# A four-layer block of scan, experts and attention on one core: normalised rows on ScalarE, shared experts as a queue behind, one copy per scatter

## The chip, the cores and the metric

The kernel runs on one core of a Trainium2 chip. The metric is the time of one execution on the device in microseconds; of the kernel before, three executions took 1660.49, 1661.27 and 1664.24 us, and their median, 1661.27 us, is the time before.

The core has five engines with queues of their own, which meet through semaphores only. The profile calls them PE (TensorE, matrix products; PEld is its loading of weights), DVE (VectorE), ACT (ScalarE), POOL (GpSimd) and SP (SyncE, which here issues DMAs). An engine works through its queue in order: an instruction that waits holds up all that stand behind it on that engine.

## The reference

The input x has 8 batches of 512 rows of 256 numbers in float32. Four layers are added to it one after the other, each on the normalised rows:

```python
x = x + _L0_attn_a_ref(_layernorm(x, axis=-1), ...)   # a scan over the 512 rows
x = x + _L0_ffn_ref(_layernorm(x, axis=-1), ...)      # a mixture of experts
x = x + _L0_attn_b_ref(_layernorm(x, axis=-1), ...)   # causal attention, 16 heads of 16
x = x + _L0_ffn_ref(_layernorm(x, axis=-1), ...)      # the same mixture, same weights
```

`_layernorm` is `(x - m) / jnp.sqrt(v + eps)`, without weights. The scan projects to 512 channels, keeps a decaying sum of each, and projects back. The attention clips its scores to -10 to 10, masks and takes a softmax. The mixture is

```python
topk_idx, tw = _route(x, router_w, bias)              # 4 of 16 experts per row, with gains
h = jnp.einsum('td,edf->etf', x, gate_w)
u = jnp.einsum('td,edf->etf', x, up_w)
y = jnp.einsum('etf,efd->etd', jax.nn.silu(h) * u, down_w)
routed = jnp.einsum('etd,te->td', y, combine)
sh = jax.nn.silu(x @ sh_gate_w) * (x @ sh_up_w) @ sh_down_w   # two shared experts, every row
return (routed + sh).reshape(hidden_states.shape)
```

## The kernel before

**Stages.** `stretch(Scan())` runs the scan layer for all 8 batches, and with it everything of the first mixture but the chosen experts: the route of every batch and the shared experts. `routed(0, ...)` then runs the chosen experts on blocks of 128 rows that were sorted by expert in HBM (`xg`). `stretch(Attention())` and `routed(1, ...)` do the same for the third and fourth layer. In `routed` a block's rows are loaded (L982 to L986), turned, multiplied (L1029, L1059) and added to `part` in HBM by an indirect DMA of GpSimd (L1069). At its start it needs the last scatter into `xg` and the table of blocks that `blocks` makes (L906, L915).

**A stretch.** Its loop takes the batches in turn. In iteration b the main work of batch b (`layer.main`) is woven together with the projection of batch b + 1 (Attention), the normalisation and turning of a coming batch (`norm(nxt)`, `turn(nxt)`), the route of batch b - 1 (`Route`: its norm, its scores and the chain of small VectorE steps in `choices`), the scatter of the sorted rows of batch b - 2, and some of the shared experts. The weaving is an order of program: `beside` lets several pieces of work advance evenly by matmul columns, and `timed` puts each step of a piece at a given fraction of the iteration. The Tile framework then fixes each engine's order from that.

**The shared experts.** `shared_experts` (L1142 for gate and up, L1170 for down) costs TensorE the same for each batch: 12 units of 1024 columns, 96 units in a stretch. `quota` says how many units stand beside an iteration: the first number holds for b = 2 to 6, the second for the last iteration, the third for the piece behind the loop, in which the last batch's route is made; what is left goes beside the final piece, with the last scatters and the table of blocks. The results are stored to `part` (L1180). The transposed rows that they read come from the route. In Scan the rows of batches 0 to 5 are kept at the end of `w_all`, in the place of the last two (`OUT`) experts' weights (`kept_rows`, three places in turn); those two experts are loaded once batch 5 is done (`done_with`). In Attention the rows stay in one of the `kb4` buffers (nine of them, shared with much else), and `w_all` from expert 5 on holds the attention's scores and projections (`spot`); these experts are loaded again after the loop (`end`).

**Normalised rows.** `normed` makes mean and variance on VectorE (L469, L470), raises the variance to -0.5 on GpSimd (L489), and forms the rows on VectorE, one instruction for each of four tiles of 128 rows (L494): subtract the mean, multiply by the factor. With `by_vector` the root is made on VectorE as well; the last route of each stretch and the two batches that `prepared` handles during `routed(0)` do so.

**Scatters.** For each route 16 indirect DMAs on GpSimd (L794) put 128 rows each into `xg`, at places that stand in `slots`. So that they do not all start at once, the places are copied to `slots` by ScalarE, in pairs (`PACE = 2`, L791): the copies are pinned in ScalarE's order, and a scatter cannot start before its copy. The last route of Attention is not paced: one VectorE copy (L773) gives all 16 places.

Of the kernel before, what the change touches and what calls it, by code (L numbers as in the profile page):

```python
# [61 lines left out]
PACE = 2  # L62
SENT = 4
# [20 lines left out]
def tile_hybrid_block(  # L84
# [351 lines left out]
    def by_shares(src, tag: str, into, into_rows: bool):  # L436


        rows = src()
        through = dram.tile([T, D], FP, name=f"through_{tag}")  # L440
        nc.sync.dma_start(out=through.rearrange("(t p) d -> p t d", p=P), in_=rows)
        share = rows.rearrange("p t d -> p (t d)") if into_rows else kb4(f"share_{tag}").rearrange("p t d -> p (t d)")
        for a in range(QUAD):
            nc.sync.dma_start(
                out=share[a * SQ : (a + 1) * SQ, :].rearrange("s (g c) -> s g c", g=T // SQ),
                in_=through[:, a * KD * SQ : (a + 1) * KD * SQ].rearrange("(g s) c -> s g c", s=SQ),
            )
        yield 0
        dst = work.tile([P, KD, T], FP, tag="kb4", name=f"xT_{tag}", bufs=KB)
        into(dst)  # L450
        for half in range(2):
            g = slice(half * T // SQ // 2, (half + 1) * T // SQ // 2)
            nc.vector.transpose(
                dst.rearrange("p k (g s) -> p k g s", s=SQ)[:, :, g],
                share.rearrange("p (g i k) -> p k g i", i=SQ, k=KD)[:, :, g],
            )
        yield 0
# [4 lines left out]
    def normed(b: int, tag: str, place, by_vector: bool = False, pinned: bool = False, past=lambda: None):  # L462
# [27 lines left out]
        xn = place()  # L490
        for t in range(NT):
            with tc.issue_after(past().ins) if past() is not None else nullcontext():
                keep(
                    nc.vector.tensor_scalar(  # L494
                        xn[:, t, :], x_sb[:, t, :], mv[:, t, 0:1], rstd[:, t : t + 1], ALU.subtract, ALU.mult
                    )
                )
            yield
# [24 lines left out]
    class Scan:  # L523
        mixture, ahead, copies, turns = 0, 1, by_scalar, (0.75, 0.79)
        quota = (10, 10, 20)
        early = 0
# [89 lines left out]
    class Route:  # L616
# [3 lines left out]
        def __init__(self, i: int, b: int, copies):  # L620
            self.i, self.b, self.tag, self.copies = i, b, f"m{i}_{b}", copies
            self.held = {}
            self.rest = choices(i, b, self.tag, self.held, i == 0 or b < B - 1)
# [11 lines left out]
        def norm(self, by_vector: bool = False):  # L635
# [3 lines left out]
            return normed(self.b, self.tag, self.place, by_vector, past=past)  # L639

        def scores(self, shares: bool = False):
            if shares:
                yield from by_shares(
                    lambda: self.held["rows"][:, :, 0:D], self.tag, lambda xnT: self.held.update(xnT=xnT), False
# [542 lines left out]
    first_expert = E - -(-(ES + QK) * NT * D // WEXP)  # L1187
# [8 lines left out]
    class Attention:  # L1196
        mixture, ahead, copies, turns = 1, 2, by_both, (0.65, 0.85)
        quota = (12, 6, 18)
# [5 lines left out]
        def done_with(self, b: int):  # L1204
            pass

        def end(self):
            for e in range(first_expert, E):
                load_expert(e)
# [207 lines left out]
    def stretch(layer):  # L1417
# [5 lines left out]
        def norm(b: int, first: bool = False):  # L1423
# [4 lines left out]
            return normed(b, f"l{i}_{b}", place, False, first)  # L1428
# [70 lines left out]
        for b in range(1 if begun else 0, B):  # L1499
# [10 lines left out]
            if b > 1:  # L1510
                shared_sum = experts(layer.quota[last])
                fill.append(shared_sum)
                pieces.append(timed(sends.pop(), 0.1, 0.14, 0.18, *spread(0.22, 0.66 if last else 0.86, NT * TK)))
            if fill:
                pieces.append(behind(*fill))
            if b > 0:
# [7 lines left out]
                if last:  # L1524
# [3 lines left out]
                        timed(some(r.rest, 3 + SENT), 0.79, 0.81, 0.83, *spread(0.85, 1.0, SENT)),  # L1528
# [18 lines left out]
            if i == 0 and b == 2:  # L1547
# [7 lines left out]
        chain = 3 + PICKS  # L1555
        issue(
# [3 lines left out]
                timed(sends.pop(), *spread(0.0, 0.5, NT * TK - SENT)),  # L1560
                timed(r.scores(), 0.2, 0.22, *spread(0.28, 0.33, NT)),
                timed(some(r.rest, chain + 8), *spread(0.36, 0.68, chain), *spread(0.7, 1.0, 8)),
# [6 lines left out]
                timed(r.rest, *spread(0.0, 0.5, NT * TK - 8)),  # L1569
# [103 lines left out]
```

## Time and profile before

| | us |
|---|---|
| median of three runs | 1661.27 |
| the profiled execution, on the device | 1663.38 |
| its span from first to last instruction | 1661.7 |
| TensorE busy | 1583.4 (95%) |
| VectorE busy | 1004.3 (60%) |
| ScalarE busy | 766.2 (46%) |
| GpSimd busy | 762.9 (46%) |
| the 256 scatters (L794), GpSimd busy | 258.4 |
| the 120 copies that pace them (L791) | 21.3 |
| matmuls of the shared experts end (Scan, Attention) | 349.9, 1266.0 |

The busy times come from one profiled execution; ends of matmuls are modelled, so a busy TensorE is not TensorE at its peak. PEclk is the share of its full clock that TensorE was granted. In a list of groups the columns are line, engine, operation, what is written from what, count, then busy time in us and mean ns of one, then the engine's idle time before them and who ended it. In a timeline a row is start, duration, engine, line and operation, with the idle time before it and its releaser in brackets. A table by stretches gives for each engine its busy us and its count of instructions.

### The profile page before, as it was taken

What the parts mean: (1) busy time and instruction counts of PE and PEld (TensorE: products, weight loads), DVE (VectorE), ACT (ScalarE), POOL (GpSimd) and SP (SyncE); (2) the same over time, 40 slices, a digit from 0 to 9 for tenths busy, and PEclk for the clock granted to TensorE, in tenths of its full rate; (3) what the DMA queues carried; (4) which work ended last, traced back from release to release, by engine and by line L of the source; (5) the groups of instructions that cost most, each with busy time, mean ns of one, the idle gap of its engine ahead of it and who ended that gap; (6) DMA issues with size and microseconds to landing.
All of it is one profiled execution on the core that took longest, in us unless ns stands there. A gap on an engine that the chain in (4) does not pass through costs nothing. (4 is left out here: it accounts for less than half of the span.)

```text
span 1661.7 us, 33893 instructions
## 1 busy us (share of the span) xinstructions
PE 1583.4 (95%) x10030; PEld 1162.3 (70%) x10030; DVE 1004.3 (60%) x3265; ACT 766.2 (46%) x1486; POOL 762.9 (46%) x639
## 2 busy tenths in 40 slices
PE   8899998999999999999999999999888999999996
PEld 5466655579999999973344444445447999999995
DVE  6777765434466444438988878868643444545553
ACT  3333432235555555556554444444113555555553
POOL 4456646525556555540032332322552555555554
PEclk9999998999999999999999999999899999999998
DMA  5444424447777766641324234232643776787776
GB/s 167 168 147 146 156 92 146 164 83 105 117 122 107 104 99 97 88 72 39 89 90 120 88 109 117 79 110 78 228 156 72 107 123 109 131 140 135 133 136 131
DMA packets 281644, 195.30 MB, mean 118 GB/s; under 512 B 168592, under 2 KB 262064, under 8 KB 281456
## 3 DMA queue, kind: packets, MB, share of 16 engines
q1 hardware_dynamic: 228896, 119.93, 28.2%
q0 software_dynamic: 51984, 72.09, 24.3%
q8 instruction: 85, 1.39, 0.4%
q10 hardware_dynamic: 576, 1.05, 0.2%
q14 instruction: 103, 0.84, 0.2%
HBM read 89.71 MB, written 103.23 MB: 116 GB/s over the span
## 5 line engine op out<-in xcount | busy, mean ns | idle before, releaser
L1069 POOL DMA_INDIRECT part<-rows x272 | 425.9, 1566 | 341.4 <-ACT rows L1068 246.0
L794 POOL DMA_INDIRECT xg<-sorted_m,slots_m x256 | 258.4, 1009 | 274.4 <-ACT slots_m L791 75.6
L1029 PEld LDWEIGHTS ph<-rows,gate 128*128 128x128 f32 x2160 | 277.6, 191 | 33.5 <-ACT rows L1012 22.0
L1029 PE MATMUL ph<-rows,gate 128*128 128x128 f32 x2160 | 291.6, 278 | 1.7 <-ACT rows L1012 1.7
L1029 PE MATMUL ph<-rows,up 128*128 128x128 f32 x2160 | 285.3, 275 | 0.0
L1059 PE MATMUL pyr<-w_all,rows 128*128 x1088 | 279.3, 380 | 0.0
L1029 PEld LDWEIGHTS ph<-rows,up 128*128 128x128 f32 x2160 | 262.9, 192 | 0.0
L1002 DVE COPY up<-w_all 128x512 f32 x270 | 119.5, 443 | 225.1 <-PE ph L1029 201.1
L1002 ACT COPY gate<-w_all 128x512 f32 x270 | 166.5, 617 | 123.7 <-DVE up L1002 59.6
L1039 DVE TENSOR_TENSOR rows<-ph,rows 128x256 f32<-128x256 f32 x272 | 115.3, 424 | 151.3 <-ACT rows L1037 80.9
L1291 ACT ACTIVATE w_all<-ps_a 128x1024 f32<-128x1024 f32 x160 | 155.1, 1021 | 104.3 <-PE ps_a L1281 97.8
L1059 PEld LDWEIGHTS pyr<-w_all,rows 128*128 128x128 f32 x1088 | 186.9, 192 | 14.3
L1068 ACT ACTIVATE rows<-pyr,gain 128x256 f32<-128x256 f32 x272 | 128.7, 473 | 77.7 <-PE pyr L1059 58.1
L1037 ACT ACTIVATE rows<-ph 128x256 f32<-128x256 f32 x272 | 104.3, 383 | 116.7 <-PE ph L1029 99.1
L1170 PE MATMUL pd_m<-sd_sb,act_m 128*128 128x256 f32 x512 | 124.5, 391 | 13.3 <-DVE act_m L1158 7.6
L1170 PEld LDWEIGHTS pd_m<-sd_sb,act_m 128*128 128x128 f32 x512 | 97.9, 195 | 40.5 <-issue 11.4
L1281 PE MATMUL ps_a<-w_all 32*128 32x384 f32 (+3 forms) x1024 | 106.6, 475 | 8.8 <-ACT w_all L1291 8.5
L1301 DVE SCALAR_TENSOR_TENSOR w_all<-w_all,causal 128x512 f32<-128x512 f32 (+1 forms) x160 | 91.5, 572 | 38.3 <-ACT w_all L1291 36.4
L1317 PE MATMUL po_a<-w_all,v_a 128*32 128x512 f32 (+3 forms) x1024 | 92.8, 452 | 0.3 <-issue 0.3
L1281 PEld LDWEIGHTS ps_a<-w_all 32*128 32x128 f32 x1024 | 45.0, 188 | 66.6 <-ACT w_all L1291 34.5
L1016 DVE STREAM_TRANSPOSE rows<-rows 128x256 f32<-128x256 f32 x180 | 78.8, 438 | 5.6 <-issue 2.6
L1142 PE MATMUL pg_m<-xT_m,sg_sb 128*128 128x512 f32 x160 | 78.0, 610 | 0.0
(223 smaller groups left out, 1937.8 us busy)
## 6 DMA issues: line engine op xcount, KB each, us to landing
rows<-xg SPq DMA_DIRECT2D x720, 32.0 KB
rows<-xg SPq DMA_DIRECT2D x92, 134.0 KB
part<-x SPq DMA_DIRECT2D x16, 512.0 KB
part<-ys_m SPq DMA_DIRECT2D x14, 512.0 KB
sum<-part SPq DMA_DIRECT2D x14, 512.0 KB
w_all<-in_L_ffn_gate_w_dram SPq DMA_DIRECT2D x27, 256.0 KB
w_all<-in_L_ffn_up_w_dram SPq DMA_DIRECT2D x27, 256.0 KB
w_all<-in_L_ffn_down_w_dram SPq DMA_DIRECT2D x27, 256.0 KB
```

The lines of the kernel that those rows point to most:

```text
L794: nc.gpsimd.indirect_dma_start(out=xg[i], out_offset=bass.IndirectOffsetOnAxis(ap=slots[:, at : at + 1], axis=0), in_=rows[:, t, :], in_of ...
L1002: copy(here, w_all[:, bass.ds(held[n][0] + half * KD * F, KD * F)])
L1029: nc.tensor.matmul(ph[s][:, f * P : (f + 1) * P], lhsT=both[s][:, k * F + f * P : k * F + (f + 1) * P], rhs=rows[:, ROW + k * P : ROW + (k ...
L1037: nc.scalar.activation(act, ph[0], AF.Silu)
L1039: made = nc.vector.tensor_mul(act, ph[1], act)
L1059: nc.tensor.matmul(py, lhsT=act[:, f * P : (f + 1) * P], rhs=w_all[:, bass.ds(w + 2 * KD * F + f * D, D)], start=(f == 0), stop=(f == KF - 1),
L1068: nc.scalar.mul(y, py, gain[:, TK : TK + 1])
L1069: acc = nc.gpsimd.indirect_dma_start(out=parts[i][n % 2], out_offset=bass.IndirectOffsetOnAxis(ap=rows[:, D + 2 * TK : D + 2 * TK + 1].bit ...
L1170: nc.tensor.matmul(py[:, j, :], lhsT=acts[n][:, f, t * P : (t + 1) * P], rhs=shared[n][3][:, f, :], start=(n == 0 and f == 0), stop=(n == ...
L1281: nc.tensor.matmul(ps[j // 2][:, j % 2, col : col + n], lhsT=k_sb[w][r, o, c * P : (c + 1) * P], rhs=q_sb[r, o, c * P : T], start=True, st ...
L1291: nc.scalar.activation(es[two], ps[two], AF.Exp, scale=ATT_SCALE)
L1317: nc.tensor.matmul(at["po", w][32 * j : 32 * j + 32, c * P : T], lhsT=v_sb[:, c, h * VC : h * VC + 32], rhs=at[w, c, j], start=(c == place ...
```

## The change

1. `normed` takes `by_scalar_too`. In Attention, for the layer's own norms (batches 2 to 7) and for routes 0 to 6, VectorE makes one small offset, minus the mean times the factor, and ScalarE forms the four tiles as Identity of factor times x plus offset.
2. Attention's quota becomes (10, 8, 20). Its transposed rows of routes 0 to 5 go to `kept_rows` at the end of `w_all`; the attention's own places move down by two experts, and the last two experts are loaded again when batch 5 of the shared experts is done.
3. `PACE` is 1, and the last route of Attention is paced too. In Scan the last 4 of a route's 16 scatters move to the first sixth of the next iteration (`over`), the other 12 spread up to 0.97; no scatter of route 6 stands in the last iteration any more (`sent`), and 4 instead of 8 of route 7's stand before the final piece (`begun_last`). Attention keeps its numbers there.

```diff
@@ -59,8 +59,7 @@
 CLIP = 10.0
 KB, COLS = 9, 6
 HALVED = 1597463007.0
-PACE = 2
-SENT = 4
+PACE = 1
 OUT, STAY = 2, 3
 AHEAD = 6
 BY_PE = 3
@@ -433,7 +432,7 @@
             copies[k](dst[:, k, :], flat)
             yield T // 2
 
-    def by_shares(src, tag: str, into, into_rows: bool):
+    def by_shares(src, tag: str, into, into_rows: bool, home=None):
 
 
         rows = src()
@@ -446,7 +445,7 @@
                 in_=through[:, a * KD * SQ : (a + 1) * KD * SQ].rearrange("(g s) c -> s g c", s=SQ),
             )
         yield 0
-        dst = work.tile([P, KD, T], FP, tag="kb4", name=f"xT_{tag}", bufs=KB)
+        dst = home() if home else work.tile([P, KD, T], FP, tag="kb4", name=f"xT_{tag}", bufs=KB)
         into(dst)
         for half in range(2):
             g = slice(half * T // SQ // 2, (half + 1) * T // SQ // 2)
@@ -459,7 +458,9 @@
     by_both = (nc.scalar.copy, nc.vector.tensor_copy)
     by_scalar = (nc.scalar.copy, nc.scalar.copy)
 
-    def normed(b: int, tag: str, place, by_vector: bool = False, pinned: bool = False, past=lambda: None):
+    def normed(
+        b: int, tag: str, place, by_vector=False, pinned=False, past=lambda: None, by_scalar_too=False
+    ):
 
         keep = tc.keep_in_program_order if pinned else lambda made: made
         x_sb = x_tiles[b]
@@ -488,6 +489,15 @@
             keep(nc.vector.tensor_scalar(rstd, mv[:, :, 1], EPS, None, ALU.add))
             powers[tag] = nc.gpsimd.tensor_tensor(rstd, rstd, neg_half, ALU.pow)
         xn = place()
+        if by_scalar_too:
+            off = small.tile([P, NT], FP, tag="minus", name=f"minus_{tag}")
+            nc.vector.scalar_tensor_tensor(off, mv[:, :, 0], -1.0, rstd, ALU.mult, ALU.mult)
+            for t in range(NT):
+                nc.scalar.activation(
+                    xn[:, t, :], x_sb[:, t, :], AF.Identity, scale=rstd[:, t : t + 1], bias=off[:, t : t + 1]
+                )
+                yield
+            return
         for t in range(NT):
             with tc.issue_after(past().ins) if past() is not None else nullcontext():
                 keep(
@@ -523,6 +533,7 @@
     class Scan:
         mixture, ahead, copies, turns = 0, 1, by_scalar, (0.75, 0.79)
         quota = (10, 10, 20)
+        over, sent, begun_last = 4, 0, 4
         early = 0
 
 
@@ -620,7 +631,7 @@
         def __init__(self, i: int, b: int, copies):
             self.i, self.b, self.tag, self.copies = i, b, f"m{i}_{b}", copies
             self.held = {}
-            self.rest = choices(i, b, self.tag, self.held, i == 0 or b < B - 1)
+            self.rest = choices(i, b, self.tag, self.held, True)
 
         def place(self):
             rows = work.tile([P, NT, ROW], FP, tag="rows", name=f"sorted_{self.tag}")
@@ -636,12 +647,18 @@
 
 
             past = (lambda: gained.get(self.b - 1)) if self.i == 0 else lambda: None
-            return normed(self.b, self.tag, self.place, by_vector, past=past)
+            return normed(
+                self.b, self.tag, self.place, by_vector, past=past, by_scalar_too=self.i == 1 and not by_vector
+            )
 
         def scores(self, shares: bool = False):
             if shares:
                 yield from by_shares(
-                    lambda: self.held["rows"][:, :, 0:D], self.tag, lambda xnT: self.held.update(xnT=xnT), False
+                    lambda: self.held["rows"][:, :, 0:D],
+                    self.tag,
+                    lambda xnT: self.held.update(xnT=xnT),
+                    False,
+                    (lambda: kept_rows(self.b)) if self.b < B - 2 else None,
                 )
                 yield from logits(self.i, self.b, self.tag, self.held)
                 return
@@ -1184,7 +1201,7 @@
 
 
 
-    first_expert = E - -(-(ES + QK) * NT * D // WEXP)
+    first_expert = E - OUT - -(-(ES + QK) * NT * D // WEXP)
     spots = {"es": [0, ES, 0], "qk": [ES, QK, 0]}
 
     def spot(kind: str, rows: int):
@@ -1195,17 +1212,17 @@
 
     class Attention:
         mixture, ahead, copies, turns = 1, 2, by_both, (0.65, 0.85)
-        quota = (12, 6, 18)
+        quota = (10, 8, 20)
+        over, sent, begun_last = 0, 4, 8
         early = 2
         norms, scores, choose = (0.0, 0.12, 0.2, 0.28), (0.29, 0.45, 0.55, 0.6), (0.66, 0.95)
         last_rows, last_scores = (0.2, 0.28), (0.35, 0.38)
         bursts, parts = {}, {}
 
-        def done_with(self, b: int):
-            pass
+        done_with = Scan.done_with
 
         def end(self):
-            for e in range(first_expert, E):
+            for e in range(first_expert, E - OUT):
                 load_expert(e)
 
         def load(self, b: int):
@@ -1425,7 +1442,7 @@
                 xn[b] = kb4(f"xn_{i}_{b}")
                 return xn[b]
 
-            return normed(b, f"l{i}_{b}", place, False, first)
+            return normed(b, f"l{i}_{b}", place, False, first, by_scalar_too=i == 1)
 
         def turn(b: int, copies=layer.copies):
             if i == 1 and b >= layer.ahead:
@@ -1510,7 +1527,14 @@
             if b > 1:
                 shared_sum = experts(layer.quota[last])
                 fill.append(shared_sum)
-                pieces.append(timed(sends.pop(), 0.1, 0.14, 0.18, *spread(0.22, 0.66 if last else 0.86, NT * TK)))
+                if len(sends) > 1:
+                    pieces.append(timed(sends.pop(0), *spread(0.0, 0.16, layer.over)))
+                wait = 0.16 if i == 0 and b == 2 else 0.0
+                first = [wait + place for place in (0.1, 0.14, 0.18)]
+                if layer.over:
+                    pieces.append(timed(some(sends[0], 3 + NT * TK - layer.over), *first, *spread(0.22 + wait, 0.97, NT * TK - layer.over)))
+                else:
+                    pieces.append(timed(sends.pop(), *first, *spread(0.22, 0.66 if last else 0.86, NT * TK)))
             if fill:
                 pieces.append(behind(*fill))
             if b > 0:
@@ -1525,7 +1549,7 @@
                     pieces += [
                         timed(r.scores(), *layer.last_scores, *spread(0.5, 0.56, NT)),
                         timed(some(r.rest, PICKS), *spread(0.57, 0.67, PICKS - 1), 0.76),
-                        timed(some(r.rest, 3 + SENT), 0.79, 0.81, 0.83, *spread(0.85, 1.0, SENT)),
+                        timed(some(r.rest, 3 + layer.sent), 0.79, 0.81, 0.83, *spread(0.85, 1.0, layer.sent)),
                     ]
                 else:
                     pieces += [
@@ -1553,20 +1577,24 @@
 
         r = start_route(B - 1)
         chain = 3 + PICKS
+        many = layer.begun_last
+        left = [timed(sends.pop(0), *spread(0.0, 0.14, layer.over))] if layer.over else []
+        within = (0.16, 0.8) if layer.over else (0.0, 0.5)
         issue(
             beside(
                 experts(layer.quota[2]),
                 timed(r.norm(by_vector=True), *spread(0.0, 0.05, 2 * NT)),
-                timed(sends.pop(), *spread(0.0, 0.5, NT * TK - SENT)),
+                *left,
+                timed(sends.pop(), *spread(*within, NT * TK - layer.sent)),
                 timed(r.scores(), 0.2, 0.22, *spread(0.28, 0.33, NT)),
-                timed(some(r.rest, chain + 8), *spread(0.36, 0.68, chain), *spread(0.7, 1.0, 8)),
+                timed(some(r.rest, chain + many), *spread(0.36, 0.68, chain), *spread(0.84 if layer.over else 0.7, 1.0, many)),
             )
         )
         table = []
         issue(
             beside(
                 Piece((B * 12 - (B - 3) * layer.quota[0] - sum(layer.quota[1:])) * each, whole),
-                timed(r.rest, *spread(0.0, 0.5, NT * TK - 8)),
+                timed(r.rest, *spread(0.0, 0.65 if layer.over else 0.5, NT * TK - many)),
                 timed(blocks(i, table), 0.03, 0.14, 0.26, 0.38),
             )
         )
```

## The prediction

> **What bounds the kernel now.** I read the page's slices first, then the table by stretches cut where the line numbers of the timeline change: 0 to 351 us is Scan, 351 to 741 the first run of sorted blocks, 741 to 1267 Attention, then the second run of blocks and the landing of its last sums.
>
> ```profile
> PE   8899998999999999999999999999888999999996
> PEclk9999998999999999999999999999899999999998
> ```
>
> ```profile
> core 0: us, PE busy (x) PEld busy (x) DVE busy (x) ACT busy (x) POOL busy (x), PEclk, DMA share, GB/s
> ...
> 241.00:280.00 39.00, 32.35 (x126) 21.67 (x125) 23.24 (x85) 10.49 (x25) 18.05 (x18) 0.87 0.21 72
> 280.00:351.00 71.00, 68.40 (x248) 40.65 (x246) 27.13 (x105) 17.80 (x40) 29.74 (x33) 1.00 0.50 156
> ...
> 794.00:840.00 46.00, 42.78 (x325) 18.79 (x322) 42.14 (x124) 23.93 (x31) 3.58 (x5) 0.96 0.31 85
> ...
> 900.00:962.00 62.00, 59.61 (x393) 29.04 (x390) 50.89 (x148) 28.34 (x45) 20.09 (x21) 1.00 0.36 107
> ...
> 1148.00:1198.00 50.00, 45.50 (x279) 19.49 (x280) 36.96 (x121) 16.76 (x33) 20.12 (x21) 0.86 0.53 181
> 1198.00:1267.00 69.00, 57.42 (x216) 35.47 (x215) 31.83 (x119) 9.41 (x21) 28.61 (x31) 0.95 0.41 132
> ```
>
> TensorE sets the time nearly everywhere; a middle iteration of Attention (900 to 962) keeps it busy 59.6 of 62 us. Its lost time lies at the ends of the two stretches. Counting idle time plus (1 - granted clock) of the stretch: 241 to 280 loses 6.7 + 5.1 = 11.7 us, 1148 to 1198 loses 4.5 + 7.0 = 11.5, 1198 to 1267 loses 11.6 + 3.5 = 15.1. I then looked at TensorE's timeline there:
>
> ```profile
> 270.38 0.69 PE L743 MATMUL pr_m<-sel_m,tri 128*128 128x64 f32 x2 [6.65 <-DVE sel_m L735]
> ```
>
> ```profile
> 1174.83 1.01 PE L1317 MATMUL po_a<-w_all,v_a 128*32 128x512 f32 x1 [0.34 <-issue]
> 1178.78 2.99 PE L1281 MATMUL ps_a<-w_all 32*128 32x128 f32 x16 [2.93 <-ACT w_all L1291]
> ```
>
> ```profile
> 1248.79 2.27 PE L906 MATMUL pe_b<-chosen_b,cand_e 128*128 128x143 f32 x8 [7.96 <-DVE chosen_b L895]
> ```
>
> Three holes: 6.7, about 3 and 8.0 us. GpSimd's timeline shows what they share: each falls in or just behind a row of scatters (L794) without a break, 1.26 us apart (0.96 busy, 0.30 issue): 16 from 250.5 to 271.8, 12 from 1159.7 to 1175.0, 16 from 1226.6 to 1246.8. In the first and third VectorE too sat idle, 5.9 us up to 267.8 and 4.7 us up to 1246.5, for a matmul that by its modelled end was long done. Why is not shown; the coincidence is what I use.
>
> **The shared experts moved back.** One batch of shared experts is 12 units; TensorE's timeline has a whole batch from 305.10 to 325.79, so a unit costs 20.7 / 12 = 1.72 us. The quota (12, 6, 18) left 12 units for the final piece; (10, 8, 20) leaves 18. Five iterations lose 2 units each, the last one gains 2, the piece behind the loop 2, the final piece 6: 10 units or 17.2 us move from the middle to the end, none vanish. What an iteration gains by it: GpSimd's pow of the routes (L489 rstd_m) stands at 794.0, 839.6, 900.3, 961.8, 1024.0, 1087.9, 1148.0, so an iteration without shared experts takes 45.6 us, one with 12 units 60 to 64, mean 62.1. That is 16.5 us for 20.7 us of work, 0.8 of it. The gain is 5 x 3.44 = 17.2 at most, 0.8 x 17.2 = 13.7 at least; I take 15.5, as TensorE is at 59.6 of 62 and the last units added weigh most. At the end 17.2 us of work come to a place with 11.5 + 15.1 = 26.6 us lost. They lengthen it by 17.2 if they meet other work, by nothing if all falls into holes. The 8.0 us hole is a wait in program order that more matmuls queued behind it do not fill unless the scatters' rows break; the 1148 to 1198 loss is partly want of work. I take half: +8.5. Attention by this part: -15.5 + 8.5 = -7, from -17.2 to +3.5.
>
> What the longer wait needs is hidden: the transposed rows of routes 0 to 5 now stay in the last two experts' place in w_all instead of kb4 buffers (same transposes), and those two experts are loaded again from HBM, 6 DMAs of 256 KB on SP behind the queue of batch 5. SP then holds only zeros and stores until the block loads at 1256, and Scan already does the same. If that cover went, the six issues (some 0.4 us each in SP's timeline) and 1.6 MB at the 132 GB/s of that stretch would be 12 us of transfer beside 1198 to 1267; 0 to +3 in my range. Each batch's store (512 KB, SP) moves with its experts; 1198 to 1267 held three, the last on GpSimd ahead of the first sum of the blocks, and holds four now (60, 72, 84 and 96 of the 96 units end there).
>
> **Normalised rows on ScalarE.** Six layer norms and seven routes of Attention, 13 x 4 = 52 rows of tiles, leave VectorE; it gets 13 small offsets.
>
> ```profile
> L494 DVE TENSOR_SCALAR sorted_m<-x,mv_m,rstd_m 128x256 f32<-128x256 f32 x64 | 23.3, 409 | 11.2 <-POOL rstd_m L489 9.5 <-issue 1.2 <-DMA xg<-sorted_m,slots_m 0.3
> L575 ACT ACTIVATE xi_s<-xi_s,d_sb 128x512 f32<-128x512 f32 x32 | 23.1, 722 | 62.1 <-DVE state_s L574 57.9 <-issue 4.2
> L791 ACT CAST slots_m<-choices_wm 128x2 uint32<-128x2 f32 x120 | 21.3, 190 | 7.6 <-DVE choices_wm L767 7.5
> ```
>
> VectorE loses 52 x 0.41 - 13 x 0.16 = 19 us of 400 busy. The trace has no such activation of 256 columns; the nearest is L575, 0.72 us for 512 with a factor per row, and from the copies of 512 and 256 columns out of PSUM (0.585, 0.37) a halving saves 0.21, so about 0.5 us, between 0.37 and 0.72. ScalarE gains 26 us (19 to 37); it is busy 28 of 62 per iteration, VectorE 51 of 62. The row speaks for the move: the engine with room takes it. The Trainium skill's page "ScalarE: Activation LUTs", section Rules for kernel authors, speaks against it: multiplications and additions belong on VectorE, which is faster per element. By that rule alone the move would lose 52 x 0.09 = 5 us; by the busy rows it costs nothing on the path. What it gains I bound by TensorE's loss in a middle iteration, 2.4 us: 0 to 1 us each over seven, I take -2 in all. Against it stands the wait added: the offset waits on VectorE for GpSimd's pow as the first normalised tile did before, and ScalarE's first row then waits for both with exps queued behind it. Cover is the three bursts by which the weights run ahead; rival 3 prices its loss. On GpSimd each pow stands among scatters that now wait one by one; a pow that has to pass one more of them is late by its spacing, some 2 us, against norms planned a fifth of an iteration (12 us) ahead of their use.
>
> **One copy per scatter.** 136 more copies of 0.19 us on ScalarE: 64 in Scan, 72 in Attention, 26 us beside work, on no path by themselves. A scatter now waits for its own place in ScalarE's order. In Scan 12 of 16 spread over three quarters of a 36 us iteration, 2.25 us apart instead of 1.4, the other 4 in the next iteration's first sixth; that breaks the 250 to 272 row. Of the 11.7 us lost in 241 to 280 I take back 5, from 0 to 11.7. The Trainium skill's "TensorE: Matmul & The Clock Gate", What's actually happening, says that an idle window of about 3.4 us halves the clock until TensorE is busy again; the clock of 0.86 and 0.87 stands only in the stretches with holes. By that rule a removed hole would also return all 5.1 us of clock there, by rows alone I cannot split it.
>
> Scan pays at its end: 12 scatters instead of 8 in the final piece, up to 0.65 instead of 0.5. Now the last scatter starts at 331.1, row loads at 336.8, VectorE turns the first rows at 346.05, the shared experts end at 349.9 and the first block's matmul starts at 351.4. The final piece (16 units, 27.5 us) starts near 322; 0.6 of it is 338.5, landing some 3 us later, then 9.3 us of loads: 351, at the edge. Cost 0 to +5, I take +1. In Attention the end has more room, since 18 units or 31 us now lie beside the last route's scatters.
>
> **Sum.** -7 - 2 - 5 + 1 = -13 us. The profiled execution took 1663.38 us (span 1661.7), the median is 1661.27; the sum is made on the profiled one, 1650, and taken off the median: 1648. About 0.2%, 3.3 us, is what can be told from no change.
>
> **Rivals.** (1) All of it works: all 17.2 us fall into holes, VectorE's relief gives 1 us in each of seven iterations, and 241 to 280 loses nothing: -17.2 - 7 - 11.7 makes 1625. For it: the holes coincide with unbroken rows of scatters. Against: coincidence, not cause. (2) The change moves time only: work moved from the middle is paid back at the end in full and scatters keep their rows, since GpSimd needs 1.26 us each and the new places after the loop (16 in 22 us) are hardly wider: 1658 to 1665. (3) Slower: ScalarE's queue. The first row of a norm stands in order ahead of exps; where it waits for pow and offset, bursts wait with it.
>
> ```profile
> DVE sorted_m L494 <- POOL rstd_m L489: 8.4, 7, 1.2
> PEld ps_a L1281 <- ACT w_all L1291: 34.5, 39, 5.2
> ```
>
> In these waits of 741 to 1267 VectorE loses up to 1.2 us per norm now, and TensorE already waits 34.5 us for exps. At 1.2 us wait plus 4 x 0.5 us work, 13 norms put 42 us between exps; it decides once over half of that reaches TensorE, more than the 15.5 won: +6 to +10 with the end half filled, 1670.
>
> **Chances.** Forecast 0.6 (1631 to 1657), (1) 0.12, (2) 0.14, (3) 0.14. Faster 0.74 (forecast, 1, little of 2), same 0.09, slower 0.17 (3 and the rest of 2). The range 1630 to 1668 leaves out most of (1) and half of (3).
>
> **What would show it.** Right: about 59 us between the routes' pows; shorter waits of TensorE at the three places; L494 down from 128 to 76 on VectorE, 52 activations near 0.5 us; scatters in Scan over 2 us apart; the second run of blocks starting near 1254 instead of 1266.8. Wrong: iterations still near 62 us, new waits of ps_a for exps behind a normalising activation, or the first block of either run waiting for row loads.

## The result and the profile after

The changed kernel takes 1669.61 us (median of 7 runs, 1666.78 to 1671.83), the kernel before 1662.75 us in 7 runs beside them. The ratio is 1.0048, 95% interval 1.003 to 1.0067: about 7 us slower, where 1648 was forecast. The profiled execution took 1669.93 us (span 1668.2; before 1663.38 and 1661.7).

The page of the changed kernel, two rows of its slices and the groups that changed most:

```profile
PE   8899998999999999999999989999999999999995
PEclk9999999999999999999999999999899999999998
...
L811 POOL DMA_INDIRECT xg<-sorted_m,slots_m x256 | 268.7, 1050 | 292.8 <-ACT slots_m L808 160.7
...
L1298 PE MATMUL ps_a<-w_all 32*128 32x128 f32 (+3 forms) x1024 | 117.7, 491 | 27.5 <-ACT w_all L1308 25.8
```

The last row is the finding in short. It is the score matmul (L1281 before), and behind the bar stands TensorE's idle time before it: 27.5 us, of which 25.8 for the exp (the exponentials of the softmax, on ScalarE) that has to free `ps_a`. In the kernel before the same row has 8.8 and 8.5:

```profile
L1281 PE MATMUL ps_a<-w_all 32*128 32x384 f32 (+3 forms) x1024 | 106.6, 475 | 8.8 <-ACT w_all L1291 8.5
```

The scatters wait for ScalarE's copy 160.7 us instead of 75.6, which goes with their new spacing. The table by stretches, cut near the same events as before (241 to 280 at the same times; columns: start and end, length, busy time of each engine, granted clock, DMA share, GB/s):

```profile
core 0: us, PE busy (x) PEld busy (x) DVE busy (x) ACT busy (x) POOL busy (x), PEclk, DMA share, GB/s
241.00:280.00 39.00, 32.94 (x128) 21.42 (x126) 20.80 (x87) 11.45 (x33) 18.48 (x19) 0.96 0.39 130
...
898.00:960.00 62.00, 57.58 (x376) 26.86 (x372) 47.94 (x142) 32.25 (x60) 20.29 (x20) 0.97 0.35 105
1143.00:1193.00 50.00, 46.99 (x303) 23.52 (x300) 36.47 (x121) 19.84 (x47) 19.95 (x21) 0.90 0.55 184
1193.00:1272.00 79.00, 72.82 (x251) 42.84 (x249) 36.28 (x122) 14.37 (x47) 28.69 (x32) 0.96 0.43 136
```

A middle iteration still takes 62 us, with two units of shared experts fewer in it; TensorE is idle 4.4 us of it instead of 2.4, and its clock is 0.97 instead of 1.00. By GpSimd's pows of the routes (L489 before, L490 after) and the first matmul of each run of blocks the span splits like this:

| step | before | after | difference | forecast |
|---|---|---|---|---|
| up to the first pow of Attention | 794.0 | 785.8 | -8.2 | -4 |
| first to seventh pow (the loop) | 354.0 | 357.4 | +3.4 | -17.5 |
| seventh pow to the second run of blocks | 118.8 | 128.9 | +10.0 | +8.5 |
| from there to the end of the span | 394.9 | 396.1 | +1.3 | 0 |

The differences make the 6.5 us by which the spans differ. The loop is where the forecast failed, by 21 us. There ScalarE has two waits that were not in it before, the first two rows (of the waits in Attention; columns: who waits for what, us in total, times, longest):

```profile
ACT xn L496 <- DVE minus_l L494: 12.5, 5, 4.0
ACT sorted_m L496 <- DVE minus_m L494: 8.6, 7, 1.4
...
PE ps_a L1298 <- ACT w_all L1308: 23.9, 23, 2.5
```

The third row stands against this one of the kernel before:

```profile
PE ps_a L1281 <- ACT w_all L1291: 8.5, 11, 2.9
```

Here is one of ScalarE's new waits, in its timeline at a layer norm of the changed kernel, then TensorE's at the same time (start, length, operation, and in brackets the idle time before it and what ended it):

```profile
858.02 0.60 ACT L1173 ACTIVATE sig_m<-pg_m 128x512 f32<-128x512 f32 x1 [1.16 <-PE pg_m L1159]
861.67 1.09 ACT L496 ACTIVATE xn<-x,minus_l,rstd_l 128x256 f32<-128x256 f32 x2 [3.06 <-DVE minus_l L494]
862.67 1.00 ACT L1308 ACTIVATE w_all<-ps_a 128x1024 f32<-128x1024 f32 x1
863.57 1.08 ACT L496 ACTIVATE xn<-x,minus_l,rstd_l 128x256 f32<-128x256 f32 x2
864.56 1.01 ACT L1308 ACTIVATE w_all<-ps_a 128x1024 f32<-128x1024 f32 x1
```

```profile
860.70 1.06 PE L1334 MATMUL po_a<-w_all,v_a 128*32 128x512 f32 x8
863.73 1.13 PE L1298 MATMUL ps_a<-w_all 32*128 32x128 f32 x6 [1.96 <-ACT w_all L1308]
865.62 1.01 PE L1298 MATMUL ps_a<-w_all 32*128 32x128 f32 x5 [0.76 <-ACT w_all L1308]
```

ScalarE stands still for 3.06 us before its first normalised row; the exps, next in its order, come behind two rows each, and TensorE waits twice. The timelines of the other engines say where the 3.06 us go: VectorE ends the statistics at 859.13, GpSimd a scatter at 860.35 and the pow at 861.44, VectorE the offset at 861.64.

### The profile page after: what moved, and what is told of

The parts are those of the page before. It is cut to its first block, busy times and chain, and to the rows that moved or that the text cites. A ratio compares the mean times of both kernels' runs of the same rounds, so it can differ in the third digit from the quotient of the medians.

```text
span 1668.2 us, 34112 instructions
## 1 busy us (share of the span) xinstructions
PE 1594.3 (96%) x10030; PEld 1167.3 (70%) x10030; DVE 988.7 (59%) x3225; ACT 805.5 (48%) x1674; POOL 773.9 (46%) x639
## 5 line engine op out<-in xcount | busy, mean ns | idle before, releaser
L811 POOL DMA_INDIRECT xg<-sorted_m,slots_m x256 | 268.7, 1050 | 292.8 <-ACT slots_m L808 160.7
L1298 PE MATMUL ps_a<-w_all 32*128 32x128 f32 (+3 forms) x1024 | 117.7, 491 | 27.5 <-ACT w_all L1308 25.8
L1298 PEld LDWEIGHTS ps_a<-w_all 32*128 32x128 f32 x1024 | 50.7, 194 | 88.1 <-ACT w_all L1308 53.9
L1159 PE MATMUL pg_m<-w_all,sg_sb 128*128 128x512 f32 x192 | 94.3, 613 | 0.0
L1159 PE MATMUL pg_m<-w_all,su_sb 128*128 128x512 f32 x192 | 93.8, 611 | 0.0
```

The lines of the kernel that those rows point to most:

```text
L811: nc.gpsimd.indirect_dma_start(out=xg[i], out_offset=bass.IndirectOffsetOnAxis(ap=slots[:, at : at + 1], axis=0), in_=rows[:, t, :], in_of ...
L1159: made = nc.tensor.matmul(dst, lhsT=w[:, k, f * P : (f + 1) * P], rhs=xnT[:, k, :], start=(k == 0), stop=(k == KD - 1),)
L1298: nc.tensor.matmul(ps[j // 2][:, j % 2, col : col + n], lhsT=k_sb[w][r, o, c * P : (c + 1) * P], rhs=q_sb[r, o, c * P : T], start=True, st ...
```

## The experiments

Each set of four kernels ran on one chip (numbers 7, 15, 15 and 12 on record), with the kernel before timed beside them: its median was 1656.06 us in set 1, 1624.71 in set 2, 1656.18 in set 3 and 1623.99 in set 4. The chip's number does not tell the two levels apart, as sets 2 and 3 have the same; what does is open. A ratio is compared within its set; across sets I compare the length of an iteration, which hardly depends on the set (with rows on VectorE 56.3 us in sets 1 and 3, 56.2 in 2 and 4). It is the mean of the four iterations between the second and the sixth pow of the routes: 62.1 us before and 62.7 after in the two profiles above. TensorE's idle time and clock are those of one iteration that ends at the fourth pow.

| set, kernel | median us | ratio (95%) | iteration us | idle us, clock |
|---|---|---|---|---|
| 1 a_rows_vector | 1636.15 | 0.9889 (0.9862 to 0.9916) | 56.3 | 0.6, 1.00 |
| 1 a_quota_old | 1667.36 | 1.008 (1.0054 to 1.0106) | 64.5 | 4.3, 1.00 |
| 1 a_pairs_attention | 1672.65 | 1.0105 (1.0076 to 1.0133) | 62.9 | 5.1, 0.95 |
| 1 a_scan_only | 1651.40 | 0.9977 (0.996 to 0.9993) | 60.2 | 1.1, 1.00 |
| 2 w_wait_alone | 1630.39 | 1.0046 (1.0028 to 1.0065) | 57.7 | 1.3, 1.00 |
| 2 w_work_alone | 1621.29 | 0.9986 (0.9975 to 0.9998) | 56.2 | 0.5, 1.00 |
| 2 a_pow_early | 1646.80 | 1.0143 (1.0122 to 1.0164) | 62.7 | 4.4, 0.95 |
| 2 rv_pairs_attention | 1616.03 | 0.9958 (0.9943 to 0.9972) | 56.2 | 0.6, 1.00 |
| 3 a_routes_vector | 1660.25 | 1.002 (1.0006 to 1.0034) | 61.1 | 3.1, 0.97 |
| 3 a_layers_vector | 1647.19 | 0.9935 (0.9912 to 0.9958) | 57.8 | 1.6, 1.00 |
| 3 a_rows_no_wait | 1663.95 | 1.0047 (1.0031 to 1.0064) | 58.1 | 1.1, 1.00 |
| 3 a_rows_vector_2 | 1637.17 | 0.9872 (0.9849 to 0.9895) | 56.3 | 0.6, 1.00 |
| 4 w_wait_and_work | 1657.49 | 1.0203 (1.0179 to 1.0228) | 63.0 | 4.5, 0.97 |
| 4 b_shared_moved | 1616.10 | 0.9952 (0.9938 to 0.9967) | 56.2 | 0.6, 1.00 |
| 4 rv_pairs_scan | 1616.01 | 0.9949 (0.993 to 0.9967) | 56.2 | 0.6, 1.00 |
| 4 before_again | 1623.18 | 0.9995 (0.998 to 1.0011) | 61.5 | 1.9, 0.97 |

**Set 1: which part costs.** Four kernels, each the changed one with a part undone.

```
a_rows_vector:     by_scalar_too=False              (both calls of normed)
a_quota_old:       Attention.quota = (12, 6, 18)
a_pairs_attention: pace = PACE if i == 0 else 2     (the last route unpaced, as before)
a_scan_only:       all three
```

> The changed kernel with the normalised rows of Attention formed by VectorE again; the moved shared experts and the single copies stay. Theory A (ScalarE's queue: the first row of a norm waits for GpSimd's pow and VectorE's offset, with exps queued behind it, 21 us of such waits on ScalarE in Attention and about 19 us more of TensorE waiting for exps): 10 to 20 us under the changed kernel, so 1650 to 1660 where the kernel before takes 1663, and iterations of Attention near 60 us. Theory B (the moved shared experts alone: TensorE has less to do in the middle but the chain of exps sets the iteration): within 3 us of the changed kernel, 1667 to 1672. Theory C (single copies and scatters): the same as B.

> The changed kernel with the shares of shared experts of before in Attention (12 in each iteration, 6 in the last, 18 behind); all else of the change stays. Theory A: the middle iterations lose the same waits, or hide part of them behind the two units put back; the end is 7 to 9 us shorter and the middle 0 to 10 us longer: 1662 to 1672. Theory B: the loss is the move's, so the stage returns to its length of before and Scan's gain of 9 us stays: 1652 to 1657.

> The changed kernel with one copy for two scatters in Attention, as before, and the last route's copy there unpaced; Scan keeps its single copies. Theory C (the 72 added copies on ScalarE stand among the exps and hold scatters): 5 to 10 us under the changed kernel, 1660 to 1665. Theories A and B: within 3 us of it, 1667 to 1672.

> The changed kernel with everything of Attention undone (rows on VectorE, the old shares, a copy for two scatters), so that Scan's part of the change is left. The first routed block started 9 us earlier in the changed kernel. If that is kept to the end, 1652 to 1656 where the kernel before takes 1663; if routed blocks or Attention give it back, 1660 to 1665.

Rows on VectorE again bring 0.9889: more than theory A asked for. The old shares leave the rows' loss in place (64.5 us against 60.2 without rows on ScalarE), and pairs of scatters leave the kernel slow, so B and C fall. The kernel without the rows is faster than both kernels of this case. Scan's part alone, 0.9977, fell between its two expectations: of 1663 it makes 1659.

**Set 2: wait or work.** On top of rows on VectorE, ScalarE gets the wait alone or the work alone; `a_pow_early` is the changed kernel, `rv_pairs_attention` is a_rows_vector.

```
w_wait_alone:  off = ...; nc.scalar.copy(seen, off)            # one 128x4 copy per norm
w_work_alone:  nc.scalar.activation(spare, x_sb[:, t, :], ..., scale=neg_half, bias=neg_half)
a_pow_early:   factor, pow and offset issued with the last bn_aggr, not with the first row
rv_pairs_attention: pace = PACE if i == 0 else 2     (the last route unpaced)
```

> Rows on VectorE (the kernel that took 0.9889 of the time before, first routed block of the second run at 1239.8 us), and in ScalarE's order, where the first row of each of the 13 norms stood, one copy of the offset, 128x4: the wait for pow and offset without the work of four rows. Theory A1 (the wait at the head of ScalarE's order is what costs): 15 to 30 us over the rows-on-VectorE kernel, ratio 0.998 to 1.007, iterations 60 to 63 us. Theory A2 (the work, 4 x 0.59 us per norm between the exps, is what costs): within 5 us of it, ratio 0.986 to 0.993, iterations 56 to 57 us.

> Rows on VectorE, and beside each row one activation of the same shape on ScalarE from x with a constant factor and offset into a spare tile (written as bfloat16), so that ScalarE has the work of 52 rows, about 31 us, with nothing to wait for. Theory A2 (work): 15 to 30 us over the rows-on-VectorE kernel, ratio 0.998 to 1.007, iterations 60 to 63 us. Theory A1 (wait): at most 8 us over it, ratio 0.988 to 0.994, iterations 56 to 58 us.

> The changed kernel with rows on ScalarE, but pow and offset issued with the last of the statistics, so a fifth of the planned gap ahead of the rows instead of in the same step as the first row. A1: the waits of ScalarE for the offset (21 us) go, and the time falls 10 to 30 us under the changed kernel, ratio 0.986 to 0.999. A2: within 5 us of the changed kernel, ratio 1.002 to 1.008.

> Rows on VectorE, the moved shared experts as in the change, and in Attention one copy for two scatters as before (the last route's unpaced): what the single copies are worth there. Against the kernel with only Scan changed (ratio 0.9977, 60.2 us an iteration) it adds the moved shared experts alone. If these are the whole of the 4.1 us by which an iteration is shorter: ratio 0.987 to 0.991, iterations 56 us. If the single copies carry part of it: ratio 0.992 to 0.998, iterations 58 to 60 us. Both theories of ScalarE's rows are silent here.

Neither theory had it: the wait alone lengthens an iteration by 1.4 us, the work alone by nothing. (Both ratios lie in the range that was named for a loss, but the medians are higher than these iterations explain, as both kernels also lengthen the first one, which has no shared experts, by 5 us.) The work alone is no clean test, though. Its rows depend on nothing late, and the planner put them elsewhere, as ScalarE's timeline of that kernel shows:

```profile
846.94 0.60 ACT L495 ACTIVATE spare_l<-x,neg_half 128x256 bf16<-128x256 f32 x1 [1.29 <-issue]
...
852.27 1.23 ACT L495 ACTIVATE spare_l<-x,neg_half 128x256 bf16<-128x256 f32 x2 [1.25 <-DVE x L166]
...
854.49 1.94 ACT L1304 ACTIVATE w_all<-ps_a 128x1024 f32<-128x1024 f32 x2 [0.43 <-PE ps_a L1294]
```

All four rows (one is among those left out) are through before the exps are due, in time when ScalarE waited anyway. `a_pow_early` missed its aim: the pow still runs from 853.91 to 854.97 us, behind a scatter, and the rows start at 855.21. ScalarE's waits for the offset are 20.0 us instead of 21.1, so A1 was not tested by it. `rv_pairs_attention` settles the single copies in Attention: 56.2 us an iteration with pairs, 56.3 (set 1) and 56.2 (set 4) with singles, so all of an iteration's gain there is the shared experts'. Its ratio, 0.9958, lay in the range that was named for the copies instead; set 4, at the same level, suggests why: Scan's part wins nothing there.

**Set 3: which norm.**

```
a_routes_vector: by_scalar_too=False in Route.norm          (layer norms stay on ScalarE)
a_layers_vector: by_scalar_too=False in the layer's norm    (routes stay on ScalarE)
a_rows_no_wait:  scale=neg_half, bias=neg_half in place of rstd and off
                 # leaves the normalisation of these rows out
a_rows_vector_2: a_rows_vector again
```

> The changed kernel with only the rows of the routes' norms back on VectorE; the layer norms' rows stay on ScalarE. Theory A (wait and work together: a norm holds the exps by the wait for its offset plus 4 x 0.59 us of rows, and TensorE pays what exceeds the lead that its weights have): the layer norm, with a wait of 3 us, pays the two holes of 3.0 and 1.3 us an iteration, so 60 to 61 us an iteration against 56.1 with all rows on VectorE. Theory A2 (rows come too late for what reads them, whichever norm it is): 58 to 60 us.

> The changed kernel with only the rows of the layer norms back on VectorE; the routes' rows stay on ScalarE. Theory A: the route's norm waits 1.2 us and works 2.4, and its one hole is 1.3 us: 57 to 57.8 us an iteration against 56.1. Theory A2: 58 to 60 us.

> The changed kernel with its 52 rows on ScalarE and read by the same consumers, but with a constant factor and offset in place of the pow's, which leaves the normalisation of Attention's rows out; pow and offset are still computed. Theory A: without the wait the rows' work fits in the lead of the exps, as it did beside rows on VectorE (56.1 us an iteration): 56 to 57.5 us. Theory A2 (rows on ScalarE reach their readers later): 60 to 63 us, as in the changed kernel.

> The changed kernel with all normalised rows on VectorE, again, on the chip of the three other kernels of this set, so that they can be compared with it: iterations of 56.1 us, and 0.988 to 0.996 of the time before.

The layer norms' rows alone cost 23.1 us (1660.25 - 1637.17), the routes' alone 10.0. They add up to 33.1; between the first blocks of the two runs the changed kernel took 929.4 us and a_rows_vector 896.9, 32.5 less. Both iterations lie at the upper end of what theory A named (61.1 for 60 to 61, 57.8 for 57 to 57.8) and outside A2's 58 to 60. The run without the wait is unclear: 58.1 us, above A's 56 to 57.5 and below A2's 60 to 63. Its rows met a new wait, 29.0 us in 14 waits of ScalarE for `x`, and without the normalisation its rows go to other experts, so its end can't be compared.

**Set 4: wait and work in the same place, and the other terms.**

```
w_wait_and_work: nc.scalar.activation(spare, x_sb[:, t, :], ..., scale=rstd, bias=off)
                 # beside each row that VectorE forms
b_shared_moved:  the kernel before, quota = (10, 8, 20), with the kept rows it needs
rv_pairs_scan:   a_rows_vector with pace = 2 if i == 0
before_again:    nothing
```

> Rows on VectorE for every reader, and beside them the same 52 rows formed once more on ScalarE from the same pow and offset into a spare tile that nobody reads (bfloat16): wait and work together on ScalarE, and no reader that could get its rows late. Theory A (what costs is the place in ScalarE's order: a wait and four rows ahead of exps): the two holes of the layer norm and the one of the route's norm come back, 61 to 64 us an iteration as in the changed kernel. Theory A2 (the rows reach their readers late): 56 to 58 us. The wait alone gave 57.5 and the work alone, which stood elsewhere in the order, 56.1.

> The kernel before with the moved shared experts alone (10, 8 and 20 in place of 12, 6 and 18, and the rows kept for them). The forecast's term: 7 us under the kernel before, ratio 0.996. If an iteration falls by 4 us as it did between the kernel with Scan's part alone (60.2) and the one with the shares and single copies on top (56.1): 18 us won in the middle, 4 to 9 given back at the end, ratio 0.991 to 0.995. If the single copies in Attention carry that gain: ratio 0.997 to 1.000.

> The changed kernel with all rows on VectorE and, in Scan, one copy for two scatters again, while the new places of the scatters there stay. If the single copies give Scan's 9 us (first routed block 342 instead of 351): 5 to 9 us over the same kernel with single copies, the first routed block at 347 to 351. If the places do: within 2 us of it, the block at 342 to 344.

> The kernel before, unchanged, for its stages on the chip of these runs: ratio 1.000; iterations of Attention 60 to 62 us by the clock of that chip, and the start of the routed blocks that the shares of the others are to be compared with.

Wait and work together, with no reader for the rows, bring the whole loss of an iteration back: 63.0 us. Late readers (A2) are out; what costs is a wait *and* rows ahead of exps in ScalarE's order. The kernel with the shared experts alone gains 8 us on the kernel before, about as forecast, and single copies in Scan are worth nothing in this set (0.9949 with pairs; first routed block at 334.7, against 334.2 in `w_wait_and_work` with singles). Neither expectation for that block, 342 to 344 or 347 to 351, was met: both came from kernels of set 1's level.

## Why the prediction was wrong, step by step

**Normalised rows on ScalarE: forecast -2, measured +26 to +33. This is the step that failed.** (By the ratios, 1.0048 against 0.9889 and 0.9872, it is 26 to 29 us; `a_pow_early` less `rv_pairs_attention` in set 2 is 30.8; the sum of set 3 is 33.1.) Two of its sentences failed: "Cover is the three bursts by which the weights run ahead", a cover whose size was never worked out, and the gain of "0 to 1 us each" from VectorE's relief. VectorE did lose the rows (L504 has 76 of the 128), but no iteration is shorter for it. What the cover is can be read where the rows are on VectorE, in ScalarE's timeline of a_rows_vector at the same layer norm:

```profile
856.93 0.60 ACT L1173 ACTIVATE sig_m<-pg_m 128x512 f32<-128x512 f32 x1 [1.16 <-PE pg_m L1159]
859.77 1.94 ACT L1308 ACTIVATE w_all<-ps_a 128x1024 f32<-128x1024 f32 x2 [2.25 <-PE ps_a L1298]
```

ScalarE is free for 2.25 us there before the scores are ready. That is the cover at this place. The changed kernel puts 3.06 us of wait and 1.09 of rows ahead of the first exp, 1.9 us more than fit, and 1.08 more ahead of the second: TensorE's two holes, 1.96 and 0.76 us. (The expectations counted the same holes as 3.0 and 1.3 us of delay.) At the route's norm the wait is 1.2 us, and one hole of 1.0 us is left. The same sum holds in two more kernels. The wait alone, 3.04 us and a copy of 0.19, is 1.0 more than fits, and makes holes of 1.06 and 0.42 us:

```profile
857.30 0.19 ACT L496 COPY seen_l<-minus_l 128x4 f32<-128x4 f32 x1 [3.04 <-DVE minus_l L494]
...
858.47 0.49 PE L1294 MATMUL ps_a<-w_all 32*128 32x128 f32 x4 [1.06 <-ACT w_all L1304]
859.38 1.14 PE L1294 MATMUL ps_a<-w_all 32*128 32x128 f32 x12 [0.42 <-ACT w_all L1304]
```

In w_wait_and_work 3.03 us of wait and 1.87 of three rows stand ahead of the first exp, 2.65 more than fit; its hole is 2.71:

```profile
864.02 1.87 ACT L498 ACTIVATE spare_l<-x,minus_l,rstd_l 128x256 bf16<-128x256 f32 x3 [3.03 <-DVE minus_l L495]
...
866.84 0.58 PE L1297 MATMUL ps_a<-w_all 32*128 32x128 f32 x4 [2.71 <-ACT w_all L1307]
```

The work alone stood elsewhere: hence no single cause in set 2. Rows at this place without any wait are shown by no run.

The other third of an iteration's loss is the clock, which the prediction had as something that a removed hole gives back, not as something that a new hole takes. The changed kernel in steps of 3 us around that layer norm:

```profile
859.00:862.00 3.00, 2.76 (x18) 0.47 (x16) 2.00 (x7) 0.33 (x1) 2.10 (x3) 1.00 0.25 92
862.00:865.00 3.00, 1.13 (x6) 0.52 (x6) 2.09 (x4) 3.00 (x6) 0.00 (x0) 0.96 0.00 0
865.00:868.00 3.00, 2.38 (x18) 1.29 (x22) 0.93 (x2) 1.37 (x4) 1.76 (x2) 0.50 0.62 221
868.00:871.00 3.00, 3.00 (x18) 1.08 (x11) 1.97 (x4) 1.48 (x4) 1.47 (x2) 0.50 0.73 186
871.00:874.00 3.00, 3.00 (x22) 1.20 (x21) 0.86 (x3) 0.94 (x3) 1.48 (x2) 0.90 1.03 294
```

After the stretch with 1.13 us of work in 3, the clock is 0.50 for 6 us. Whole iterations of four kernels, each between its third and fourth pow (changed kernel; rows on VectorE; wait alone; wait and work):

```profile
898.35:960.30 61.95, 57.53 (x373) 26.86 (x373) 47.93 (x141) 32.20 (x60) 20.29 (x20) 0.97 0.35 104
```

```profile
889.70:945.90 56.20, 55.60 (x376) 26.23 (x374) 50.11 (x147) 28.54 (x53) 20.38 (x21) 1.00 0.38 115
```

```profile
889.30:946.50 57.20, 55.90 (x373) 26.51 (x373) 50.62 (x149) 28.66 (x54) 20.03 (x20) 1.00 0.37 113
```

```profile
900.80:962.90 62.10, 57.65 (x373) 27.18 (x374) 50.91 (x149) 32.77 (x60) 19.93 (x21) 0.97 0.34 104
```

The changed kernel loses 4.4 - 0.6 = 3.8 us more to idling and 0.03 x 62 = 1.9 us to the clock, together the 5.7 by which it is longer. The wait alone leaves 1.3 us idle in the iteration and the clock at 1.00; so do the routes' rows alone (1.6 us). The Trainium skill's "TensorE: Matmul & The Clock Gate", section What's actually happening, ties the half clock to an idle window of about 3.4 us. No hole of these iterations is that long; 1.96 and 0.76 us idle with 1.13 us of work between them were enough. Nor does the size of the hole alone decide. The kernel before, in set 4, has the same single hole of 1.9 us in four iterations, at 868.3, 929.0, 991.3 and 1052.0; at the second and fourth the clock fell, at the first and third it did not. The first and second in steps of 3 us:

```profile
868.00:871.00 3.00, 1.11 (x8) 0.52 (x10) 2.87 (x7) 0.00 (x0) 1.24 (x2) 1.00 0.12 46
871.00:874.00 3.00, 3.00 (x26) 2.42 (x23) 2.61 (x7) 1.98 (x3) 0.00 (x0) 1.00 0.01 3
...
929.00:932.00 3.00, 1.14 (x6) 0.52 (x10) 2.87 (x8) 0.00 (x0) 0.95 (x1) 0.85 0.13 46
932.00:935.00 3.00, 3.00 (x20) 2.06 (x21) 1.40 (x3) 1.04 (x2) 0.00 (x0) 0.58 0.00 0
```

In a_quota_old a pair of 1.13 and 1.00 us did it in one of four iterations. What decides is open; the holes of the changed kernel lowered the clock in every iteration from the second to the fifth (0.95 to 0.97).

The size of a row was under-rated too: 0.592 us measured, 0.5 taken, inside the 0.37 to 0.72. The page of before has a nearer row than L575, which the prediction overlooked: L1068, an activation of 128x256 out of PSUM with one factor per row, 473 ns. The Trainium skill's "ScalarE: Activation LUTs", section What ACT_TABLE_LOAD costs, gives 186 ns plus 0.833 ns per element plus 93 ns for each operand that holds one number per row, an estimate of 585 ns here; the trace's 592 agree.

**Rival 3** had this mechanism and its outcome, 1670, at a chance of 0.14. Its inner numbers were different: it put 1.2 us of wait before every norm, and ScalarE waited up to 4.0 us at the layer norms; it reached 1670 without the clock and with a smaller gain of the shared experts to be eaten up. That the number fits to the microsecond is luck; that the queue decides is not.

**Shared experts moved: forecast -7, measured -7.8** (0.9952 of 1624) in b_shared_moved. The net is right, partly by luck, as both parts were too small and their misses partly cancel. The loop from the first to the seventh pow fell from 350.2 to 328.7 us, -21.5 for the 15.5 taken; the end grew from 102.2 to 114.0, +11.8 for 8.5 (in the two profiles, of which that of b_shared_moved is its fastest execution). The iteration fell by 5.3 us (61.5 to 56.2), 3.44 of it the two units. Most of the rest is a wait that I had left out, TensorE's for the products of shared experts in the kernel before, with the clock that it costs in two of four iterations:

```profile
870.15 0.70 PE L1170 MATMUL pd_m<-sd_sb,act_m 128*128 128x256 f32 x2 [1.89 <-DVE act_m L1158]
```

In Attention these waits were 7.8 us of TensorE before and 1.0 with the shares moved. At the end, the hole of 8.0 us ahead of the block table, which more work was not to fill, is gone in the changed kernel, whose longest there is 2.85 us. But in set 4 the kernel before has no hole above 1.6 us between the seventh pow and the blocks either: neither the 8.0 us nor the 2.9 that the prediction read at that end belong to the program alone.

**One copy per scatter in Scan: forecast -5 + 1, measured at the first routed block -8.8 in the runs of the result (351.4 to 342.6), +1.4 to +4 in set 4.** The size was near, the reason was not. I took back part of 241 to 280 because its hole lay behind an unbroken row of scatters. In set 4 the kernel before has the same row, 1.26 us apart, and no such hole. VectorE's wait for the projection, in the kernel before in the two (the first is the profile that the prediction read):

```profile
267.81 0.69 DVE L520 TENSOR_TENSOR x<-py_s,x 128x512 f32<-128x512 f32 x1 [5.94 <-remote]
```

```profile
253.77 0.69 DVE L520 TENSOR_TENSOR x<-py_s,x 128x512 f32<-128x512 f32 x1 [0.61 <-PE py_s L511]
```

By TensorE's records these matmuls end at 262.0 and 253.7 (modelled ends). In the first profile VectorE started 5.8 us later, released by something that the profile can't name (`remote`), in the other at once; TensorE then waited 6.65 us and its clock fell to 0.50, in the other 0.89 us at 1.00. The kernels with the first block at 342 to 345 (sets 1 and 3) all have a hole of 4.4 to 4.5 us at the same matmuls, the changed kernel of the result one of 4.6; the kernels of sets 2 and 4, changed ones at 334 to 335, all have 0.9. So this hole goes with the set, neither with the copies nor with their pairing.

Nor did most of the 8.8 us come from there. The score step of that route, ahead of the hole, ran at 257.3 before and 249.7 after: 7.6 us were won by then, and the hole gave 2. The kernel before had lost time earlier, in waits of the same unnamed kind, VectorE's longest this one:

```profile
86.62 0.32 DVE L676 STREAM_TRANSPOSE logit_m<-pl_m 128x128 f32<-128x128 f32 x1 [9.46 <-remote]
```

Up to the first block VectorE and ScalarE have 8 such waits of over 1.5 us in that profile, 2 in the changed kernel, and none in any of the eight kernels of sets 2 and 4. What stands behind them is open, and so is how much of the 8.8 us the new places saved by it. In set 4 they save nothing: the first block starts at 334.2 to 334.7 with them, at 332.8 and 330.6 without. So at the level of sets 2 and 4 the rows' loss shows in full: `a_pow_early`, whose waits are nearly those of the changed kernel, is at 1.0143 there.

**What would show it wrong** was named rightly: iterations near 62 us and new waits of `ps_a` for exps. The third sign, a first block that waits for row loads, did not come up in the changed kernel.

## What to carry to other kernels

Before work is moved to an engine "with room", look at the place in that engine's order and not at its busy share: price the time for which the first moved instruction waits plus the work that stands with it ahead of the next instruction on the path, against the idle time that the engine has at that very place. Where the sum exceeds it, the rest reaches TensorE, and the clock can charge it again (here 1.9 us on top of 3.8). And two events that coincide in one profile, such as a row of scatters and a hole, are worth one look at the same program in another set of runs before a gain is booked on them.

## What was not expected of the hardware

- Two idle stretches of TensorE, 1.96 and 0.76 us with 1.13 us of work between, brought the granted clock to 0.50 for some 6 us. A single one of 1.89 us lowered it in two iterations of one profile (0.85 and 0.58 over the next 6 us) and left it at 1.00 in two others; 1.06 and 0.42 us with 0.49 between left it at 1.00.
- One program differs locally from set to set: the kernel before took 1656 us in sets 1 and 3 and 1624 in sets 2 and 4, and all three holes that the prediction read (6.65, 2.9 and 8.0 us) are absent or at 0.89 us in set 4. Sets 2 and 3 carry the same chip number.
- VectorE started 5.8 us after the recorded (modelled) end of the matmuls that it read, released by nothing that the profile names; in the stretches of Scan and Attention such waits of over 1.5 us stand only in profiles of sets 1 and 3 and of the result. Whether the matmuls ended late or another wait was met is not shown.
